# Sums of the V weights' blocks placed sooner; one add for four heads' exponentials, and the first unit's block sums between the rotary products

## The chip, the cores and the metric

The kernel runs on one core of one Trainium2 chip. A core has five engines, each with its own queue of instructions that it works through in order: TensorE (PE in the profile), VectorE (DVE), ScalarE (ACT), GpSimd (POOL) and SyncE (SP, which here issues the DMAs). They wait for each other on semaphores. The metric is the device time of one execution in microseconds. The kernel before took 2176.2 us (median of three runs, 2175.44 to 2180.79).

## The reference

Two transformer layers follow each other on 16 sequences of 256 tokens and 256 channels, all in float32. Each layer has self-attention, cross-attention to a context, and a feed-forward block, every one behind a layer norm whose factor and shift come from a condition vector. Layer 0 has 16 heads of 64 channels with rotary turns of the queries and keys; layer 1 has 16 heads of 16 channels. Cut to what matters here, the attention of layer 0 is:

```python
def _attn(xq, ctx, wq, wkv, wo, bo):
    q = _heads(xq @ wq)
    k, v = jnp.split(ctx @ wkv, 2, axis=-1)
    k = _heads(k)
    v = _heads(v)
    q = _rope(q, sq, cq)
    k = _rope(k, sk, ck)
    sim = jnp.einsum('bhnd,bhmd->bhnm', q, k) * DH ** (-0.5)
    a = jax.nn.softmax(sim, axis=-1)
    o = jnp.einsum('bhnm,bhmd->bhnd', a, v)
    return o.transpose(0, 2, 1, 3).reshape(xq.shape[0], xq.shape[1], MID) @ wo + bo
```

In the self-attention of layer 0 `ctx` is the normed input itself, so V is the product of a 256 x 256 input and a 256 x 1024 matrix of weights.

## The kernel before, in words

The work is cut into 96 jobs: six phases (layer 0 self-attention, cross-attention, feed-forward, then the same of layer 1) of 16 sequences each. A job of attention has two steps, s = 0 and s = 1; a step handles two units of four heads. The loop over `steps` writes the instructions of every engine out in an order made by hand, and nothing reorders them: an instruction stands in its engine's queue where the loop puts it, and what it needs from other engines it waits for.

**A step of layer 0.** At its end the step before has put the scores of this step's two units into PSUM (`scores`, `stage_s`, matmuls of line 657), and ScalarE takes their exponentials, two heads at a time (line 670), so that a unit has two tiles `pr` of 128 x 1024. The denominators of the softmax come by VectorE: `stage_t` adds the two halves of the keys of two heads (line 679, one add for each `pr`), `stage_turn` transposes the sum in blocks of 32 (line 685), `stage_reduce` sums each block (line 692). TensorE meanwhile makes the queries and keys of the next step in four parts, `rotary(then, e, half)`, with e the unit. After each part VectorE multiplies the result by cosines and sines (two instructions of line 614, tiles `m`), and after the second part of a unit GpSimd makes the turned queries and keys, tiles `qk`, by one subtraction and one addition (line 622). There are two buffers for each kind of `m`, so the second unit's multiplications wait until GpSimd has read the first unit's. `layer0_sums` multiplies the exponentials with V (line 727). Then `scores` of the next step follows: it overwrites the PSUM banks that the rotary products stood in, so it needs all eight multiplications of line 614, and `qk` of both units.

**Order of VectorE in a step**, where nothing else comes between: add, add, transpose of the first unit; two multiplications; first add of the second unit; two multiplications; second add; four multiplications; block sums of the first unit; transpose and block sums of the second. After that in s = 1 come the additions to the residual `x` (lines 1018 to 1025, in `finish_folded`, for the job before) and the norm of a later job (lines 364 and 374); in s = 0 the moments of a later one.

**Seven products in place of eight.** In the first phase V of jobs 2 and later is made with Strassen's scheme (`by_seven`, `value_part`): seven block products with sums of blocks of the weights and of the tokens. The sums of the weights are made once, by four GpSimd instructions (`fold_value_weights`, lines 519 to 522; one of them writes over a block of `wv` itself, so the plain products of jobs 0 and 1 must be done). Five more sums, of blocks of the output weights, are made once in a phase (`fold_weights`, line 995), for `finish_folded`. Both calls stand at the end of step s = 1 of job 0. The sums of the tokens are made for each job (`fold_tokens`, lines 532 to 535) at the head of step s = 0 of the job before. TensorE's second product in that step (`value_part(nxt, 0)`, block product 5) needs the first of them.

**Buffers.** The tiles with tag `pr` come from four buffers of 128 x 1024; the feed-forward jobs take theirs, `sums` in `pair_hidden`, from the same four.

Of the kernel before, what the change touches and what calls it, by code (L numbers as in the profile page):

```python
# [10 lines left out]
F32 = mybir.dt.float32  # L11
# [32 lines left out]
def fast(ctx: ExitStack, tc: tile.TileContext, a: dict, out: bass.AP, flag):  # L44
# [222 lines left out]
    def wtile(shape, tag, name, bufs=1):  # L267
        return wpool.tile(shape, F32, tag=tag, name=name, bufs=bufs)
# [375 lines left out]
    def stage_s(job, u, at):  # L644

        key = job["key"]
        pair = job["qk"].pop(u)
        for t in range(NT):
            for half in range(2 if job["layer"] == 0 else 1):
                for g, h in [(g, h) for g in range(2) for h in range(4)]:  # L650
                    r = slice(32 * h, 32 * h + 32)
                    keys = slice(t * P + 64 * g, t * P + 64 * g + 64)
                    if job["layer"] == 0:
                        lhs, rhs = pair[half][r, 1, keys], pair[half][r, 0, :]
                    else:
                        lhs, rhs = pair[1][r, keys], pair[0][r, :]
                    nc.tensor.matmul(  # L657
                        banks[64 * g : 64 * g + 64, at + h, t * N : (t + 1) * N], lhs, rhs,
                        start=(half == 0 and (t == 0 or job["layer"] == 1)),
                        stop=(half == 1 or job["layer"] == 1), skip_group_check=(job["layer"] == 0),  # L660
                    )
        prs = []
        for p in range(2):
            pr = work.tile([P, 2, NT, N], F32, tag="pr", name=f"pr_{key}_{u}_{p}", bufs=4)
            sc = banks[:, at + 2 * p : at + 2 * p + 2, :].rearrange("p h (t n) -> p h t n", n=N)

            parts = 2 if job["layer"] == 1 and u % 2 == 0 and p == 0 else 1
            for i in range(parts):
                one = slice(i, i + 1) if parts == 2 else slice(0, 2)
                nc.scalar.activation(pr[:, one], sc[:, one], AF.Exp, scale=0.125 if job["layer"] == 0 else 0.25)  # L670
            prs.append(pr)
        job["pr"][u] = prs

    def stage_t(job, u, p):

        pr = job["pr"][u][p]
        if p == 0:
            job["both"] = work.tile([P, 4, N], F32, tag="both", name=f"both_{job['key']}_{u}", bufs=1)
        nc.vector.tensor_tensor(job["both"][:, 2 * p : 2 * p + 2, :], pr[:, :, 0, :], pr[:, :, 1, :], ALU.add)  # L679

    def stage_turn(job, u):

# [35 lines left out]

    def layer0_sums(job, u, at):

        key, v, prs = job["key"], job["v"], job["pr"].pop(u)
        o = bank(at, 2, N)
        for half in range(2):
            for t in range(NT):
                for h in range(4):
                    col = (4 * u + h) * 64 + 32 * half
                    nc.tensor.matmul(  # L727
                        o[32 * h : 32 * h + 32, half, :], v[:, t, col : col + 32], prs[h // 2][:, h % 2, t, :],
                        start=(t == 0), stop=(t == NT - 1),
                    )  # L730
        if u % 2 == 0:
            job["halves"].append(work.tile([P, 4, N], F32, tag="part", name=f"raw_{key}_{u}", bufs=4))
        raw = job["halves"][-1][:, 2 * (u % 2) : 2 * (u % 2) + 2, :]
        nc.scalar.copy(raw, o)  # L734
        job["raw"].append(raw)

    def layer1_sums(job, c, e, at):

        key, v, prs = job["key"], job["v"], job["pr"].pop(2 * c + e)
        o = bank(at, N)  # L740
        for t in range(NT):
            for h in range(4):
                nc.tensor.matmul(  # L743
                    o[32 * h : 32 * h + 32], v[:, t, 4 * c + h, 32 * e : 32 * e + 32],
                    prs[h // 2][:, h % 2, t, :], start=(t == 0), stop=(t == NT - 1),
                )

        if c == 0 and e == 0:  # L750
            job["parts"].append(work.tile([P, 4, N], F32, tag="part", name=f"oT_{key}", bufs=4)[:, 0:2, :])
            job["sums"] = work.tile([P, N], F32, tag="inv", name=f"sums_{key}")
        raw, sums = job["parts"][0][:, c, :], job["sums"]
        if e == 0:
            nc.scalar.activation(raw, o, AF.Copy, scale=mask[:, 0:1])
        else:
            nc.vector.scalar_tensor_tensor(raw, o, mask[:, 1:2], raw, ALU.mult, ALU.add)
        eighth = mask[:, 4 - 2 * e + c : 5 - 2 * e + c]
        if c == 0 and e == 0:
            nc.scalar.activation(sums, o, AF.Copy, scale=eighth)  # L760
        else:
            nc.vector.scalar_tensor_tensor(sums, o, eighth, sums, ALU.mult, ALU.add)
# [99 lines left out]
    def pair_hidden(job, pair, part):  # L862
# [3 lines left out]
        mine = slice(2 * half, 2 * half + 2)  # L866
        if part == 0:
            job["places"] = x, y, z = [bank(next_bank(), 2, N) for _ in range(3)]
            job["sums"] = [work.tile([P, 2, 2, N], F32, tag="pr", name=f"sums{i}_{key}", bufs=4) for i in range(2)]
            copy, six = (job["sums"][0][:, i] for i in range(2))  # L870
            block_products(job, x, 1, True)
            block_products(job, y, 6, True)
            block_products(job, z, 5, True)
            nc.scalar.copy(copy, x)
            nc.vector.tensor_tensor(six, y, copy, ALU.add)
            if half == 0:
                for one in pair:
# [9 lines left out]
        copy, six = (job["sums"][0][:, i] for i in range(2))  # L887
        seven = job["sums"][1][:, 0]
# [95 lines left out]
        for t in (1, 0):  # L984
            nc.sync.dma_start(out=out[job["b"]][t * P : (t + 1) * P], in_=x[:, t, :])

    def fold_weights(ph):
        w = ph["w"]["wo"]
        b = [[w[:, 4 * k : 4 * k + 4, n * P : (n + 1) * P] for n in range(2)] for k in range(2)]
        folded = ph["folded"] = {2: b[0][0], 5: b[1][1]}  # L990
        for m, x, y, op in ((1, b[0][0], b[1][1], ALU.add), (3, b[0][1], b[1][1], ALU.subtract),
                            (4, b[1][0], b[0][0], ALU.subtract), (6, b[0][0], b[0][1], ALU.add),
                            (7, b[1][0], b[1][1], ALU.add)):
            folded[m] = wtile([P, 4, P], "folded", f"folded_w_{m}", 5)
            nc.gpsimd.tensor_tensor(folded[m], x, y, op)  # L995

# [175 lines left out]
    for i, (j, s) in enumerate(steps):  # L1172
# [123 lines left out]
        elif layer0:  # L1296
            then = attention(i + 1, 0)
            if leaving and s == 1 and nxt["kind"] == "ffn":
                fold_input_weights(nxt["phase"], nc.gpsimd)
            if s == 0 and by_seven(nxt):  # L1300
                fold_tokens(nxt, nc.gpsimd)
                stage_t(job, 0, 0)
                stage_t(job, 0, 1)
                stage_turn(job, 0)
                rotary(then, 0, 0)
                stage_t(job, 1, 0)
                rotary(then, 0, 1)
                sum_up(late, 5)
                if make_mod:
                    make_mod["mod"] = make_mod["make_mod"](6)  # L1310
                value_part(nxt, 0)
                stage_t(job, 1, 1)
                rotary(then, 1, 0)
                value_part(nxt, 1)
                rotary(then, 1, 1)
                stage_reduce(job, 0)
                value_part(nxt, 2)
                layer0_sums(job, 0, 5)
                value_part(nxt, 3)
# [2 lines left out]
                value_part(nxt, 4)  # L1322
                stage_reduce(job, 1)
            else:
                stage_t(job, 2 * s, 0)
                stage_t(job, 2 * s, 1)
                stage_turn(job, 2 * s)
                rotary(then, 0, 0)
                stage_t(job, 2 * s + 1, 0)
                rotary(then, 0, 1)  # L1330
                if late is not None and s == 1 and then:
                    fold_inner(late, nc.gpsimd, 7, 6)
# [13 lines left out]
                stage_reduce(job, 2 * s + 1)  # L1346
            if late is not None and s == 1:
# [14 lines left out]
            else:  # L1362
# [657 lines left out]
```

## Time and profile before

| what | value |
| --- | --- |
| median of three runs | 2176.2 us (2175.44 to 2180.79) |
| the profiled execution, its own time | 2174.1 us |
| its span, first to last instruction | 2172.3 us |
| TensorE's mean granted clock | 0.997 |
| TensorE busy | 2145.4 us of the span |
| VectorE, ScalarE, GpSimd busy | 1701.7, 878.2, 1282.5 us |
| adds of exponentials (line 679) | 256, mean 875 ns |
| GpSimd's `qk` (line 622) | 256, mean 1382 ns |
| block sums (line 692) | 128, mean 1213 ns |

The profile is one execution. A line of a timeline gives start and duration in microseconds, engine, source line, operation, tiles written and read, their shapes, how many instructions of the kind follow each other, and in square brackets how long the engine sat idle before and what released it. A view of waits adds such idle times up by the pair of waiting and releasing line: total, number, longest. A merged row runs from its first instruction's start to its last one's end, so the row itself says where its engine was next free. Spans of GpSimd are rough.

### The profile page before, as it was taken

To read this page: it belongs to the slowest core of one execution; us is meant where nothing else is said; L and a number is where in the kernel's file an instruction comes from. 1 tells how busy PE (TensorE), PEld (TensorE's weight loads), DVE (VectorE), ACT (ScalarE), POOL (GpSimd) and SP (SyncE) were. 2 spreads that over 40 slices of the span, in tenths; PEclk is the share of its full clock that TensorE was granted. 3 is DMA by queue.
4 is the path that set the end of the run, shared out by engine and by line. 5 is a ranking of instruction groups with operands and counts; after the bars stand their busy time and mean duration, and the time that the engine had idled before them with its cause. 6 is when DMAs were issued, how large, how long until landed. Compare 5 with 4: busy or idle time off the path is not lost.

```text
span 2172.3 us, 110056 instructions
## 1 busy us (share of the span) xinstructions
PE 2145.4 (99%) x50000; PEld 1412.5 (65%) x50000; DVE 1701.7 (78%) x3136; ACT 878.2 (40%) x1376; POOL 1282.5 (59%) x1234
## 2 busy tenths in 40 slices
PE   9899999999999999999999999999999999999998
PEld 5466666666665665666666667877565656566887
DVE  6687887877888999888889887774777777777875
ACT  3233333333333233333333334443666666665442
POOL 3766767767766867677676767662222323335673
PEclk9999999999999999999999999999999999999999
DMA  6011011011124221121211123221221232223221
GB/s 194 24 28 37 23 28 37 23 28 37 26 66 113 66 55 47 40 62 35 59 42 43 43 60 99 58 44 24 66 43 38 49 102 62 52 53 81 73 66 39
DMA packets 307029, 117.67 MB, mean 54 GB/s; under 512 B 243364, under 2 KB 289784, under 8 KB 306424
## 3 DMA queue, kind: packets, MB, share of 16 engines
q1 hardware_dynamic: 306008, 110.02, 20.5%
q8 instruction: 393, 6.44, 1.3%
q14 instruction: 84, 0.69, 0.1%
q10 hardware_dynamic: 544, 0.52, 0.1%
HBM read 77.14 MB, written 33.29 MB: 51 GB/s over the span
## 4 chain that ended last, share of the span: by engine, by line
PE 89%; DVE 4%; POOL 3%; DMA 1%; issue 1%; SPq 1%; ACT 0%; DVEq 0%; POOLq 0%; ACTq 0%
PE banks L82 57%; PE banks L657 15%; PE banks L727 9%; PE banks L743 5%; PE banks L593 1%; PE banks L502 1%; DVE m L614 1%; POOL raw L716 1%; POOL qk L622 1%; POOL folded L929 0%; DMA spread<-sums_seen 0%; DMA fetched<-turned 0%; SPq L214 0%; POOL folded_w L995 0%; POOL folded L1004 0%
## 5 line engine op out<-in xcount | busy, mean ns | idle before, releaser
L670 ACT ACTIVATE pr<-banks 128x1024 f32<-128x1024 f32 x576 | 487.5, 937 | 426.2 <-PE banks L657 222.4
L622 POOL TENSOR_TENSOR qk<-m,m 128x512 f32<-128x512 f32 x256 | 348.4, 1382 | 268.4 <-DVE m L614 245.6
L614 DVE TENSOR_TENSOR m<-banks,rope 128x512 f32<-128x512 f32 x512 | 324.7, 679 | 118.0 <-POOL qk L622 74.2
L679 DVE TENSOR_TENSOR both<-pr 128x512 f32<-128x512 f32 x256 | 221.4, 875 | 39.6 <-ACT pr L670 39.5
L657 PE MATMUL banks<-qk 32*64 32x256 f32 x8192 | 240.8, 378 | 2.9 <-DVE x L1021 2.0
L727 PE MATMUL banks<-pr,v 128*32 128x256 f32 x4096 | 236.2, 379 | 0.0
L734 ACT COPY raw<-banks 128x512 f32<-128x512 f32 x128 | 75.2, 587 | 390.4 <-PE banks L727 378.2
L657 PEld LDWEIGHTS banks<-qk 32*64 32x64 f32 x8192 | 184.8, 131 | 62.9 <-issue 28.1
L727 PEld LDWEIGHTS banks<-pr,v 128*32 128x32 f32 x4096 | 133.2, 110 | 100.5 <-issue 16.8
L716 POOL TENSOR_TENSOR raw<-raw,spread 128x512 f32<-128x512 f32 x128 | 161.5, 1297 | 13.4 <-DMA spread<-sums_seen 13.1
L785 POOL TENSOR_TENSOR oT<-oT,spread 128x256 f32<-128x256 f32 x64 | 45.7, 736 | 206.2 <-DVE spread L784 206.2
L685 DVE STREAM_TRANSPOSE squares<-both 128x1024 f32<-128x1024 f32 x128 | 159.3, 1244 | 3.9
L692 DVE TENSOR_REDUCE rows<-squares 128x32 f32<-128x1024 f32 x128 | 155.3, 1213 | 1.7
L452 POOL TENSOR_TENSOR x<-x,bo_b 128x256 f32<-128x256 f32 x96 | 72.8, 778 | 121.5 <-DVE xh L364 121.5
L1004 POOL TENSOR_TENSOR folded<-raw,raw 128x512 f32<-128x512 f32 x90 | 138.7, 1568 | 2.4
L82 PE MATMUL banks<-hT,wk_sa 128*32 128x256 f32 x2048 | 135.2, 382 | 0.1
L82 PE MATMUL banks<-hT,wq_ca 128*32 128x256 f32 x2048 | 134.4, 379 | 0.0
L743 PE MATMUL banks<-pr,wide_v 128*32 128x256 f32 x2048 | 134.3, 379 | 0.0
L82 PE MATMUL banks<-hT,wq_sa 128*32 128x256 f32 x2048 | 133.9, 379 | 0.0
L960 DVE TENSOR_TENSOR x<-banks,x 128x256 f32<-128x256 f32 (+2 forms) x150 | 79.6, 531 | 63.0 <-PE banks L82 56.8
L657 PE MATMUL banks<-q,k 32*64 32x256 f32 x4096 | 128.3, 381 | 0.0
L356 POOL TENSOR_TENSOR rstd<-ve,neg_half 128x2 f32<-128x2 f32 x95 | 67.6, 711 | 99.4 <-DVE ve L354 95.7
(246 smaller groups left out, 4047.4 us busy)
## 6 DMA issues: line engine op xcount, KB each, us to landing
turned<-blocks SPq DMA_DIRECT2D x380, 64.0 KB
fetched<-turned SPq DMA_DIRECT2D x380, 64.0 KB
spread<-sums_seen SPq DMA_DIRECT2D x128, 128.0 KB
x<-in_x SPq DMA_DIRECT2D x16, 256.0 KB
fetched_c<-turned_c SPq DMA_DIRECT2D x64, 64.0 KB
cT<-in_ctx_turned SPq DMA_DIRECT2D x16, 256.0 KB
out<-x SPq DMA_DIRECT2D x15, 256.0 KB
ctx<-in_ctx SPq DMA_DIRECT2D x16, 192.0 KB
```

What stands on the lines that cost most here:

```text
L82: nc.tensor.matmul(out[cut], lhsT[:, cut], rhs, start=start, stop=stop, **more)
L614: nc.vector.tensor_tensor(m, pq, rope[:, s : s + 1, :].to_broadcast([P, 2, N]), ALU.mult)
L622: nc.gpsimd.tensor_tensor(r, x, y, (ALU.subtract, ALU.add)[out])
L657: nc.tensor.matmul(banks[64 * g : 64 * g + 64, at + h, t * N : (t + 1) * N], lhs, rhs, start=(half == 0 and (t == 0 or job["layer"] == 1)) ...
L670: nc.scalar.activation(pr[:, one], sc[:, one], AF.Exp, scale=0.125 if job["layer"] == 0 else 0.25)
L679: nc.vector.tensor_tensor(job["both"][:, 2 * p : 2 * p + 2, :], pr[:, :, 0, :], pr[:, :, 1, :], ALU.add)
L685: nc.vector.transpose(job["squares"].rearrange("p b k -> p (b k)"), job.pop("both").rearrange("p h n -> p (h n)"))
L692: nc.vector.tensor_reduce(job["rows"][:, u, :], job.pop("squares"), AX.X, ALU.add)
L716: nc.gpsimd.tensor_tensor(part, part, spread[:, u : u + 1, :].to_broadcast([P, 2, N]), ALU.mult)
L727: nc.tensor.matmul(o[32 * h : 32 * h + 32, half, :], v[:, t, col : col + 32], prs[h // 2][:, h % 2, t, :], start=(t == 0), stop=(t == NT - 1),
L743: nc.tensor.matmul(o[32 * h : 32 * h + 32], v[:, t, 4 * c + h, 32 * e : 32 * e + 32], prs[h // 2][:, h % 2, t, :], start=(t == 0), stop=(t ...
L1004: eng.tensor_tensor(folded[m], *sums[m])
```

## The change

Three things are done.

The exponentials of a unit get one tile of 128 x 2048 in place of two (two buffers of it in place of four of half the size; `sums` of the feed-forward jobs likewise), and `stage_t` adds the two halves of the keys for all four heads in one instruction. ScalarE's exponentials stay as they are. In the order of a step, the one add of the second unit stands where its second add stood.

`stage_reduce` of the first unit is put directly behind the second unit's add, ahead of `rotary(then, 1, 0)`.

`fold_value_weights`, and two of the five sums of `fold_weights`, for the first phase, are put at the head of step s = 1 of job 0 in place of its end. The other three stay there. In the second phase all five stay.

```diff
-        prs = []
+        whole = job["pr"][u] = work.tile([P, 4, NT, N], F32, tag="pr", name=f"pr_{key}_{u}")
         for p in range(2):
-            pr = work.tile([P, 2, NT, N], F32, tag="pr", name=f"pr_{key}_{u}_{p}", bufs=4)
+            pr = whole[:, 2 * p : 2 * p + 2]
...
-    def stage_t(job, u, p):
-
-        pr = job["pr"][u][p]
-        if p == 0:
-            job["both"] = work.tile([P, 4, N], F32, tag="both", name=f"both_{job['key']}_{u}", bufs=1)
-        nc.vector.tensor_tensor(job["both"][:, 2 * p : 2 * p + 2, :], pr[:, :, 0, :], pr[:, :, 1, :], ALU.add)
+    def stage_t(job, u):
+
+        pr = job["pr"][u]
+        both = job["both"] = work.tile([P, 4, N], F32, tag="both", name=f"both_{job['key']}_{u}", bufs=1)
+        nc.vector.tensor_tensor(both, pr[:, :, 0, :], pr[:, :, 1, :], ALU.add)
...
-            job["sums"] = [work.tile([P, 2, 2, N], F32, tag="pr", name=f"sums{i}_{key}", bufs=4) for i in range(2)]
-            copy, six = (job["sums"][0][:, i] for i in range(2))
+            job["sums"] = work.tile([P, 4, 2, N], F32, tag="pr", name=f"sums_{key}")
+            copy, six = (job["sums"][:, 2 * i : 2 * i + 2, 0, :] for i in range(2))
...
-    def fold_weights(ph):
+    def fold_weights(ph, which):
...
+            if m not in which:
+                continue
...
+            if job["p"] == 0 and job["b"] == 0 and s == 1:
+                fold_value_weights(job["phase"], nc.gpsimd)
+                fold_weights(job["phase"], (1, 3))
             if s == 0 and by_seven(nxt):
                 fold_tokens(nxt, nc.gpsimd)
-                stage_t(job, 0, 0)
-                stage_t(job, 0, 1)
+                stage_t(job, 0)
                 stage_turn(job, 0)
                 rotary(then, 0, 0)
-                stage_t(job, 1, 0)
                 rotary(then, 0, 1)
                 sum_up(late, 5)
...
                 value_part(nxt, 0)
-                stage_t(job, 1, 1)
+                stage_t(job, 1)
+                stage_reduce(job, 0)
                 rotary(then, 1, 0)
                 value_part(nxt, 1)
                 rotary(then, 1, 1)
-                stage_reduce(job, 0)
                 value_part(nxt, 2)
...
             else:
-                stage_t(job, 2 * s, 0)
-                stage_t(job, 2 * s, 1)
+                stage_t(job, 2 * s)
                 stage_turn(job, 2 * s)
                 rotary(then, 0, 0)
-                stage_t(job, 2 * s + 1, 0)
                 rotary(then, 0, 1)
...
-                stage_t(job, 2 * s + 1, 1)
+                stage_t(job, 2 * s + 1)
+                stage_reduce(job, 2 * s)
                 rotary(then, 1, 0)
                 rotary(then, 1, 1)
...
                 for e in range(2):
                     layer0_sums(job, 2 * s + e, 4 + e if then else e)
-                stage_reduce(job, 2 * s)
                 stage_turn(job, 2 * s + 1)
                 stage_reduce(job, 2 * s + 1)
...
                 if job["b"] == 0:
-                    fold_weights(job["phase"])
-                    if job["p"] == 0:
-                        fold_value_weights(job["phase"], nc.gpsimd)
+                    fold_weights(job["phase"], (4, 6, 7) if job["p"] == 0 else (1, 3, 4, 6, 7))
```

The matmuls that read exponentials (`layer0_sums`, `layer1_sums`) read the same elements out of the larger tile.

More of the change, by code (lines that the diff above doesn't have):

```diff
@@ L670, in stage_s @@
                 nc.scalar.activation(pr[:, one], sc[:, one], AF.Exp, scale=0.125 if job["layer"] == 0 else 0.25)
-            prs.append(pr)
-        job["pr"][u] = prs
-    def stage_t(job, u, p):
-        pr = job["pr"][u][p]
-        if p == 0:
-            job["both"] = work.tile([P, 4, N], F32, tag="both", name=f"both_{job['key']}_{u}", bufs=1)
-        nc.vector.tensor_tensor(job["both"][:, 2 * p : 2 * p + 2, :], pr[:, :, 0, :], pr[:, :, 1, :], ALU.add)
+    def stage_t(job, u):
+        pr = job["pr"][u]
+        both = job["both"] = work.tile([P, 4, N], F32, tag="both", name=f"both_{job['key']}_{u}", bufs=1)
+        nc.vector.tensor_tensor(both, pr[:, :, 0, :], pr[:, :, 1, :], ALU.add)
     def stage_turn(job, u):
@@ L719, in layer0_sums @@
     def layer0_sums(job, u, at):
-        key, v, prs = job["key"], job["v"], job["pr"].pop(u)
+        key, v, pr = job["key"], job["v"], job["pr"].pop(u)
         o = bank(at, 2, N)
@@ L727, in layer0_sums @@
                     nc.tensor.matmul(
-                        o[32 * h : 32 * h + 32, half, :], v[:, t, col : col + 32], prs[h // 2][:, h % 2, t, :],
+                        o[32 * h : 32 * h + 32, half, :], v[:, t, col : col + 32], pr[:, h, t, :],
                         start=(t == 0), stop=(t == NT - 1),
@@ L737, in layer1_sums @@
     def layer1_sums(job, c, e, at):
-        key, v, prs = job["key"], job["v"], job["pr"].pop(2 * c + e)
+        key, v, pr = job["key"], job["v"], job["pr"].pop(2 * c + e)
         o = bank(at, N)
@@ L744, in layer1_sums @@
                     o[32 * h : 32 * h + 32], v[:, t, 4 * c + h, 32 * e : 32 * e + 32],
-                    prs[h // 2][:, h % 2, t, :], start=(t == 0), stop=(t == NT - 1),
+                    pr[:, h, t, :], start=(t == 0), stop=(t == NT - 1),
                 )
@@ L886, in pair_hidden @@
         x, y, z = job["places"]
-        copy, six = (job["sums"][0][:, i] for i in range(2))
-        seven = job["sums"][1][:, 0]
+        copy, six = (job["sums"][:, 2 * i : 2 * i + 2, 0, :] for i in range(2))
+        seven = job["sums"][:, 0:2, 1, :]
         (top, bottom), (top2, bottom2) = ([h[:, mine, :] for h in one["halves"]] for one in pair)
@@ L985, in finish_last @@
             nc.sync.dma_start(out=out[job["b"]][t * P : (t + 1) * P], in_=x[:, t, :])
-    def fold_weights(ph):
+    def fold_weights(ph, which):
         w = ph["w"]["wo"]
         b = [[w[:, 4 * k : 4 * k + 4, n * P : (n + 1) * P] for n in range(2)] for k in range(2)]
-        folded = ph["folded"] = {2: b[0][0], 5: b[1][1]}
+        folded = ph.setdefault("folded", {2: b[0][0], 5: b[1][1]})
         for m, x, y, op in ((1, b[0][0], b[1][1], ALU.add), (3, b[0][1], b[1][1], ALU.subtract),
```

## The prediction

> **What bounds the kernel now.** I read the page's busy times first, then the waits of TensorE, then the timelines around the waits that are long.
>
> ```profile
> PE 2145.4 (99%) x50000; PEld 1412.5 (65%) x50000; DVE 1701.7 (78%) x3136; ACT 878.2 (40%) x1376; POOL 1282.5 (59%) x1234
> ```
>
> ```profile
> PE banks L82 <- POOL tokens L532: 10.8, 1, 10.8
> PE banks L657 <- DVE x L1021: 2.0, 2, 1.0
> ...
> PE banks L657 <- DVE x L1025: 0.6, 2, 0.3
> ```
>
> TensorE is busy for all but 27 us of the 2172.3 us span, and the change takes no matmul away. So it can gain only what TensorE waits. One wait, met once, is 10.8 us: for the first sum of the tokens' blocks. The next two rows belong together: at 682.9 and 839.98 us the scores waited 1.0 us for an addition to the residual, and 0.3 us more for a later one, 1.3 us each time. The rest is the start, the end, and single waits that no edit touches.
>
> The timelines of GpSimd and TensorE show what the long wait hangs on:
>
> ```profile
> 60.41 2.52 POOL L622 TENSOR_TENSOR qk<-m,m 128x512 f32<-128x512 f32 x2 [1.49 <-DVE m L614]
> 64.30 1.53 POOL L452 TENSOR_TENSOR x<-x,bo_sa 128x256 f32<-128x256 f32 x2 [1.38 <-DVE xh L364]
> 65.81 1.52 POOL L426 TENSOR_SCALAR hT<-fetched,fac_a,add_a 128x256 f32<-128x256 f32 x1
> 67.29 7.07 POOL L995 TENSOR_TENSOR folded_w<-wo_sa 128x512 f32<-128x512 f32 x5
> 74.33 1.26 POOL L519 TENSOR_TENSOR sums_of_weights<-wv_sa 128x512 f32<-128x512 f32 x1
> ...
> 78.34 1.26 POOL L522 TENSOR_TENSOR sums_of_weights<-wv_sa,sums_of_weights 128x512 f32<-128x512 f32 x1
> 79.56 0.45 POOL L532 TENSOR_TENSOR tokens<-hT 128x128 f32<-128x128 f32 x1
> ```
>
> ```profile
> 68.23 1.04 PE L82 MATMUL banks<-wv_sa,hT 128*32 128x512 f32 x8
> 80.07 1.93 PE L82 MATMUL banks<-wv_sa,tokens 128*32 128x512 f32 x8 [10.79 <-POOL tokens L532]
> ```
>
> TensorE was ready at 69.28 us. GpSimd had nine sums of weights ahead of the tokens, from 67.29 to 79.6 us. In steady state nothing of this kind shows: the jobs of the first phase follow each other every 40.46 us and those of the second every 38.42 us (most of the pieces in the chain of work repeat at that distance).
>
> **The V weights' sums, and two of the five others, moved.** At the new place GpSimd has done its work of step 0 at 46.1 us (the small power of line 356) and sits idle until the `qk` of 56.10 us, 10.0 us by that row's bracket. Six sums start there. They follow each other every 1.33 us (74.33, 75.66, 77.00, 78.34), so they end at 46.1 + 6 x 1.33 = 54.1 us, before that `qk`. One of them overwrites a block of V weights: TensorE's last plain product with it ended at 46.8 us, and this sum is the second, at 47.4 us. They issue no DMA, and SP's queue is not passed. What is left behind `hT` is three sums.
>
> They are not quite alone. VectorE's add of exponentials and GpSimd's sums get in each other's way:
>
> ```profile
> 50.99 0.69 DVE L679 TENSOR_TENSOR both<-pr 128x512 f32<-128x512 f32 x1 [0.22 <-ACT pr L670]
> ...
> 71.74 1.51 DVE L679 TENSOR_TENSOR both<-pr 128x512 f32<-128x512 f32 x1
> ```
>
> The first ran with GpSimd idle, the second beside a sum of weights. In the second case GpSimd's sum ended at 72.70, the add at 73.25, and the next sum took 1.70 us where its neighbours took 1.26 to 1.28: first one works, then the other. So each add costs GpSimd roughly its own length, and waits itself for at most one GpSimd instruction.
>
> Now the sum. In step 1 of job 0 the first add starts when the second exponential is done, 50.97 us, waits for a sum (to about 51.4), and ends at about 52.6; transpose 1.2, four multiplications 2.4, second add 1.2, block sums 1.2, four multiplications 2.5: the last multiplication ends at 61.2 to 61.9 us, where it ended at 60.23. TensorE's scores begin at 61.05 us now, so they wait up to 0.9 us, and `qk` of the second unit comes about 1.1 us later. This is not added to the path, since GpSimd's chain ends later still: `x` at 64.1 to 64.5, then 1.53, then `hT` and the next job's first add after one another, to about 67.5; three sums of 1.28 to 71.3; the second add, 1.2, which by the rows above gets in before the tokens; 0.45 for the tokens: TensorE can go on at 73.0 us where it went on at 80.07. That gains **7.0 us**. If the second add comes behind the first tokens, it is 8.3; if another 1 us of adds falls on GpSimd, 6.0. TensorE is then still waiting about 2.5 us there. Behind this place everything moves up together: the reciprocals' transfer (`spread`) is needed about 7 us sooner, but it was issued at about 72 us and its readers began at 91.6.
>
> **The one add of four heads.** No row shows an add of 128x1024. From below: the block sums over as many elements, with one input, take 1.21 us; from above: two adds, 1.34 us alone, or 3.34 us for a pair beside GpSimd (1014.83 us). Alone I take the lower end, 1.2 us, as the nearest row. So VectorE saves about 0.14 us on a unit, 128 units, 18 us in all, on an engine that is not the bound. In return the first add waits for the second exponential, which comes 0.9 us after the first. Neither is worth anything by itself: TensorE waits for no add of this kind, it reads the exponentials themselves.
>
> **Block sums between the rotary products.** They stand where VectorE now sits idle until GpSimd has read the first unit's `m`, and the four multiplications behind them are what the next scores need:
>
> ```profile
> 1024.19 2.54 DVE L614 TENSOR_TENSOR m<-banks,rope 128x512 f32<-128x512 f32 x4 [1.18 <-POOL qk L622]
> ...
> 1027.85 2.52 POOL L622 TENSOR_TENSOR qk<-m,m 128x512 f32<-128x512 f32 x2
> ...
> 1031.24 3.71 PE L657 MATMUL banks<-qk 32*64 32x256 f32 x128
> ```
>
> The idle time is 1.18 us, the block sums 1.21. From the end of the second pair of multiplications to the end of the last took 4.32 us (1022.41 to 1026.73); it becomes 1.2 + 1.2 + 2.5 = 4.9, that is 0.6 more, or up to 1.2 if GpSimd's `qk` is held up by the whole add. Against that the second pair ends sooner, as one add of 0.67 is gone from ahead of it. So the multiplications end between 0.7 us sooner and 1.2 us later. They have 4.5 us to the scores here, and `qk` of the second unit ends at 1030.37, 2.7 us before the second half of the scores at 1033.1; no repeated step has less. Nothing is lost there.
>
> What follows the multiplications on VectorE comes sooner, for the 1.2 us of block sums are gone from there. That is what the two waits of 1.3 us are for. In both steps the addition stands at the end of multiplications, block sums, transpose, block sums. At 675.20 the multiplications waited 3.73 us for `qk`, so add and block sums fit in, and the addition is 1.2 us sooner; at 832.26 they waited 1.18, and it is 0.6 to 1.3 sooner. I take both as 1.2 saved, **2.4 us**; at the least 1.0, at the most 2.6.
>
> One step has no room: step 0 of the last job of cross-attention of layer 0, with no V products of a next job between sums and scores. TensorE waited 0.27 us there for `qk` (1278.67). Its multiplications ended at 1275.95; worked through as above they end 0.2 to 1.5 us later, and I take 0.6: **minus 0.6 us**.
>
> The Trainium skill, page "SBUF — State Buffer", section "Who interferes with whom", says that a VectorE instruction with two inputs in SBUF and a GpSimd instruction that reads SBUF lock each other out, whichever starts first keeping the shared port for its whole length. The 1.51 and 1.70 us above agree. It speaks against one long add: it would hold `qk` for all of 1.2 us where the 0.63 us add now costs it 0.5 (3.06 against 2.53 us for the pair at 284.96). By that rule the last step loses 1.5 in place of 0.6, and the whole gain is 7.9.
>
> **The larger tile.** Both halves of a unit are read up to the same four matmuls, so one buffer of twice the size comes free when the two did; `sums` likewise. Nothing gained or lost.
>
> **Sum.** 7.0 + 2.4 - 0.6 = 8.8 us, so the profiled execution's 2174.1 becomes 2165.3. The median of the runs shown stands 2.1 us above that execution, and I add the difference: 2167.4.
>
> **Rivals.** *Only the long wait shrinks* (0.22): the lock holds `qk` for the whole add in every step, VectorE's tail comes no sooner, the two waits stay, the last step loses 1.5: 7.0 - 1.5 = 5.5 us gained, 2170.7. For it: 0.6 and 1.2 are nearly one size. Against it: the idle 3.73 us at 675.20 is there to be filled. *The sums can't start early* (0.03): if something not seen kept GpSimd from them until about 50 us, `qk` would start 2 us late and the scores with it, 4 us gained, 2172. Against it: 10.0 us idle and all inputs loaded long before. *The second unit's multiplications come too late in every step* (0.05): the place is `qk` of the second unit in the step s = 1 of cross-attention, fifteen times; it decides from 2.7 us of delay on, and each further us costs 15. At 3.7 us of delay 15 us are lost against 8.8 gained, 2182.4. Against it: I find 1.2 us at the most.
>
> **Numbers.** The forecast has 0.70; its own ends are 6.0 + 1.0 - 1.5 = 5.5 and 8.3 + 2.6 - 0.2 = 10.7 gained, 2165.5 to 2170.7. Runs of one kernel lie some 2 us apart (2174.1 to 2176.2, one higher), which I add below: 2163 to 2171, taking in the first rival. A difference of 0.3%, 6.5 us, is about what can be told from none. Of the forecast 0.70 and of the first rival 0.07 gain more: faster 0.77; the rest of the first rival and the second, 0.18, the same; the third, 0.05, slower.
>
> **What will show it.** TensorE's wait for `tokens` should be 1 to 4 us in place of 10.8, and six sums of GpSimd stand between 46 and 55 us. The add of 128x1024 should have a median near 1.2 us. The two waits for the residual should be gone or under 0.5 us, and the wait for `qk` near 1270 grow to about 0.9 us. The jobs' distances of 40.46 and 38.42 us should stay. If a distance grew, the third rival holds; if the long wait stayed above 5 us, the second; if a new wait came up in every job of layer 0, I have missed who stands behind the add.

## The result, and the profile after

The changed kernel took 2162.94 us (median of four runs, 2162.62 to 2164.62), the kernel before 2175.82 us in the same comparison (four runs, 2175.31 to 2180.79): a ratio of 0.9942, 95% interval 0.9929 to 0.9955. By the medians 12.9 us were gained, by the two profiled executions 11.5 us (2174.1 to 2162.62). The forecast had 8.8 us and 2167.4 us. The measured median stands at the low edge of the range given (2163 to 2171), 0.06 us under it, and both gains are larger than the 10.7 us that the forecast's own terms allowed at most.

The page's busy times, and from the view of TensorE's waits the rows that answer to those of before:

```profile
PE 2141.6 (99%) x50000; PEld 1411.8 (65%) x50000; DVE 1656.1 (77%) x3008; ACT 878.3 (41%) x1376; POOL 1323.4 (61%) x1234
```

```profile
PE banks L82 <- POOL tokens L532: 2.3, 1, 2.3
...
PE banks L82 <- ACT pr L670: 1.3, 2, 1.2
...
PE banks L657 <- POOL qk L622: 0.5, 2, 0.3
...
PE banks L657 <- DVE x L1024: 0.3, 1, 0.3
```

The wait for tokens went from 10.8 to 2.3 us. Of the waits for the residual 0.3 us is left. A new one stands there: 1.2 us for exponentials, at one place. VectorE has 128 instructions less and 46 us less work. GpSimd's busy time grew by 41 us with the same number of instructions; 29 us of it are `qk`'s, of a mean of 1494 ns in place of 1382, since its spans hold more waiting beside the longer add.

Next, how far the same matmuls of TensorE came forward, by the starts in both timelines:

| TensorE reaches | before, us | after, us | sooner by |
| --- | --- | --- | --- |
| scores at the end of the first step | 46.92 | 46.40 | 0.52 |
| scores behind the first seven products | 93.55 | 83.88 | 9.67 |
| first keys behind the first wait for the residual | 685.76 | 674.50 | 11.26 |
| first keys behind the second | 842.82 | 828.58 | 14.24 |
| scores of layer 1's first job | 1497.18 | 1483.10 | 14.08 |
| the projection behind them | 1499.09 | 1486.26 | 12.83 |
| layer 1's feed-forward, third pair | 1988.66 | 1977.28 | 11.38 |
| end | 2172.3 | 2160.8 | 11.5 |

The first 0.52 us is the start of the run (input rows that landed sooner), not the change. So the kernel gained 9.15 us around the V sums and some 4.6 us in the attention of layer 0, and lost 1.25 us at layer 1's start and about 1.3 us in the last phase. In between the jobs follow each other as before, every 40.46 us in the first phase and every 38.42 us in the second. GpSimd around the V sums, after:

```profile
43.89 1.28 POOL L519 TENSOR_TENSOR sums_of_weights<-wv_sa 128x512 f32<-128x512 f32 x1
45.78 1.27 POOL L520 TENSOR_TENSOR wv_sa<-wv_sa 128x512 f32<-128x512 f32 x1 [0.61 <-PE banks L82]
...
49.72 3.52 POOL L994 TENSOR_TENSOR folded_w<-wo_sa 128x512 f32<-128x512 f32 x2
55.88 3.38 POOL L622 TENSOR_TENSOR qk<-m,m 128x512 f32<-128x512 f32 x2 [2.65 <-DVE m L614]
...
63.48 1.52 POOL L452 TENSOR_TENSOR x<-x,bo_sa 128x256 f32<-128x256 f32 x2 [0.23 <-DVE xh L364]
64.99 1.53 POOL L426 TENSOR_SCALAR hT<-fetched,fac_a,add_a 128x256 f32<-128x256 f32 x1
66.48 3.75 POOL L994 TENSOR_TENSOR folded_w<-wo_sa 128x512 f32<-128x512 f32 x3
70.19 1.45 POOL L532 TENSOR_TENSOR tokens<-hT 128x128 f32<-128x128 f32 x1
```

The six sums stand where GpSimd was idle, and still leave it 2.65 us before `qk`. They begin at 43.89 us, sooner than the 46.1 of the forecast (with the V sums alone it is 46.45): step 0's block sums had moved too, so what stands behind them, down to the small power of line 356, came sooner. The second of them did wait, 0.61 us, for TensorE's last plain product with the block that it overwrites. The pair of 49.72 took 3.52 us, not 2.6, and the first tokens 1.45 us, not 0.45: in each an add of VectorE stood beside it. TensorE behind the wait:

```profile
71.69 1.06 PE L82 MATMUL banks<-wv_sa,tokens 128*32 128x512 f32 x8 [2.32 <-POOL tokens L532]
72.57 1.05 PE L82 MATMUL banks<-hT,wk_sa 128*32 128x256 f32 x16
```

Before, those eight products took 1.93 us (a row that the prediction shows) and the next sixteen 1.51. The view by stretches of time gives the granted clock behind PE, PEld, DVE, ACT and POOL's busy times. Before:

```profile
80.00:81.00 1.00, 0.93 (x8) 0.28 (x12) 0.00 (x0) 0.00 (x0) 0.92 (x4) 0.50 0.00 0
...
83.00:84.00 1.00, 1.00 (x28) 0.53 (x24) 0.00 (x0) 0.00 (x0) 0.83 (x1) 1.00 0.00 0
```

and after:

```profile
72.00:73.00 1.00, 1.00 (x16) 0.39 (x12) 0.45 (x1) 0.00 (x0) 1.00 (x4) 1.00 0.18 62
```

So the long wait had a second cost. TensorE went on at half its clock until 82.7 us: from the wait's end to the scores it took 13.48 us (80.07 to 93.55), after the change 12.19 (71.69 to 83.88), 1.29 us less.

VectorE in the step of the second wait for the residual, after:

```profile
816.37 1.20 DVE L676 TENSOR_TENSOR both<-pr 128x1024 f32<-128x1024 f32 x1
817.50 1.21 DVE L689 TENSOR_REDUCE rows<-squares 128x32 f32<-128x1024 f32 x1
818.76 2.53 DVE L614 TENSOR_TENSOR m<-banks,rope 128x512 f32<-128x512 f32 x4
...
824.39 0.69 DVE L1020 TENSOR_TENSOR x<-banks,x 128x512 f32<-128x512 f32 x1
```

Add and block sums stand without a gap ahead of the four multiplications, and the addition to the residual ends at 825.08 us, where TensorE's scores had started at 824.95.

The new wait, in ScalarE's timeline of before and then of after:

```profile
1495.19 1.28 ACT L670 ACT_TABLE_LOAD   x1
1498.35 3.83 ACT L670 ACTIVATE pr<-banks 128x512 f32<-128x512 f32 x5 [1.89 <-PE banks L657]
```

```profile
1484.32 1.28 ACT L670 ACT_TABLE_LOAD   x1 [3.23 <-PE banks L657]
1485.61 3.84 ACT L670 ACTIVATE pr<-banks 128x512 f32<-128x512 f32 x5
```

The table of the exponential is loaded between the last Gelu of layer 0 and the first exponential of layer 1. Before, the load ran in idle time and the exponential waited for the scores; now the load itself stands behind that wait.

### The profile page after: what moved, and what is told of

Its sections match the earlier page's. It is cut to its first block, busy times and chain, and to the rows that moved or that the text cites. A ratio compares the mean times of both kernels' runs of the same rounds, so it can differ in the third digit from the quotient of the medians.

```text
span 2160.8 us, 109747 instructions
## 1 busy us (share of the span) xinstructions
PE 2141.6 (99%) x50000; PEld 1411.8 (65%) x50000; DVE 1656.1 (77%) x3008; ACT 878.3 (41%) x1376; POOL 1323.4 (61%) x1234
## 4 chain that ended last, share of the span: by engine, by line
PE 93%; POOL 3%; DVE 2%; DMA 1%; SPq 1%; issue 1%; ACT 0%; POOLq 0%; DVEq 0%; ACTq 0%
PE banks L82 59%; PE banks L657 16%; PE banks L724 10%; PE banks L740 5%; PE banks L593 2%; PE banks L502 1%; POOL qk L622 1%; POOL folded L926 0%; SPq L389 0%; DVE m L614 0%; DMA fetched<-turned 0%; POOL folded L1003 0%; POOL folded_w L994 0%; SPq L379 0%; POOL raw L713 0%
## 5 line engine op out<-in xcount | busy, mean ns | idle before, releaser
L622 POOL TENSOR_TENSOR qk<-m,m 128x512 f32<-128x512 f32 x256 | 377.1, 1494 | 212.9 <-DVE m L614 205.6
L614 DVE TENSOR_TENSOR m<-banks,rope 128x512 f32<-128x512 f32 x512 | 319.5, 678 | 37.7 <-PE banks L82 24.8
L676 DVE TENSOR_TENSOR both<-pr 128x1024 f32<-128x1024 f32 x128 | 172.3, 1346 | 104.2 <-ACT pr L670 102.3
```

What stands on the lines that cost most here:

```text
L614: nc.vector.tensor_tensor(m, pq, rope[:, s : s + 1, :].to_broadcast([P, 2, N]), ALU.mult)
L622: nc.gpsimd.tensor_tensor(r, x, y, (ALU.subtract, ALU.add)[out])
L676: nc.vector.tensor_tensor(both, pr[:, :, 0, :], pr[:, :, 1, :], ALU.add)
```

## The experiments

Each was run in turn with the kernel before on the same chip; the median of that one is given with it. The ratio, with its 95% interval, is estimated from all runs of both, so it is not exactly the quotient of the two medians. Where a difference is under 2 us, the runs' scatter hides it, and the place in the trace decides.

**The V sums alone.**

```diff
+            if job["p"] == 0 and job["b"] == 0 and s == 1:
+                fold_value_weights(job["phase"], nc.gpsimd)
+                fold_weights(job["phase"], (1, 3))
...
-                    fold_weights(job["phase"])
-                    if job["p"] == 0:
-                        fold_value_weights(job["phase"], nc.gpsimd)
+                    fold_weights(job["phase"], (4, 6, 7) if job["p"] == 0 else (1, 3, 4, 6, 7))
```

> Before, with only the four V sums and two of the five others moved to the head of step 1 of job 0. My account: TensorE's wait for the first tokens falls from 10.8 us to 2 to 3.5 us, and its clock stays at full speed behind it, so by the fourth job's start some 9.3 us are gained (8 from the wait, 1.3 from the clock); the two waits for the residual (1.3 us each by the profile) stay, and nothing changes in layer 1. Time 9 to 10 us under before. Rival, that the port lock of the old, shorter adds eats the gain: 6 to 7 us.

2167.93 us against 2177.75, ratio 0.996 (0.9946 to 0.9974). TensorE's waits:

```profile
PE banks L82 <- POOL tokens L532: 2.9, 1, 2.9
PE banks L82 <- DVE inner L843: 2.6, 1, 2.6
...
PE banks L657 <- DVE x L1023: 1.1, 2, 0.8
```

By the medians 9.8 us were gained, as expected. The long wait falls as in the whole change, and the waits for the residual stay, though smaller. In the profiled execution the clock didn't stay full: its record shows half clock for 3.41 us at this place, and so 7.2 us were gained by the scores there, not the 9.3 expected. Another 2.4 us went at 1977 us, in the last phase, where a wait of 2.6 us for `inner` met a second spell of 3.41 us; no part of the edit is near. The five runs agree with a clock that differs from one execution to the next: at a mean granted clock of 1.000 they took 2166.39 and 2167.0 us, at 0.999 2167.93, at 0.998 2168.76 (the profiled one) and 2169.32.

**The block sums alone.**

```diff
+                stage_reduce(job, 2 * s)
                 rotary(then, 1, 0)
                 rotary(then, 1, 1)
...
-                stage_reduce(job, 2 * s)
```

and likewise in the branch of the seven products.

> Before, with only the block sums of the first unit moved ahead of the second unit's rotary products; two adds for each unit as before, V sums late. My account: the additions to the residual come about 1.2 us sooner, both waits of TensorE for them vanish, 3 to 4 us gained; the long wait of 10.8 us stays. Rival, that the block sums only take the place of idle time if the adds are one instruction: 0 to 1 us gained, the waits stay.

2170.3 us against 2177.75, ratio 0.997 (0.996 to 0.9979). TensorE's waits:

```profile
PE banks L82 <- POOL tokens L532: 9.7, 1, 9.7
...
PE banks L657 <- DVE x L1025: 0.3, 1, 0.3
```

The waits for the residual are gone but for 0.3 us with two adds, so the rival falls. The gain is more than the 3 to 4 us expected: 7.5 us by the medians, 4.6 us by the two profiled executions, from behind the run's start to TensorE's last product. The trace puts 1.26 us of it at the first of the two waits and 2.21 at the second; and 0.76 us between 749 and 762 us and 0.67 us in the first phase, in steps where the view of waits shows no idle time before.

**The one add alone.** The larger tile and the one add, as in the change; block sums and V sums as before.

> Before, with only one tile for four heads and one add; block sums and V sums where they were. My account: VectorE saves time but nobody waits for it: the two waits for the residual shrink by less than 0.7 us each, and the first exponentials of layer 1 get the 1.2 us wait of TensorE that the changed kernel shows (the load of the exponential's table standing behind the wait for the scores). Between 1 us faster and 1.5 us slower than before. Rival, that the add is what frees VectorE: 2 us or more faster.

2176.97 us against 2177.75, ratio 1.0001 (0.9992 to 1.0011). TensorE's waits:

```profile
PE banks L82 <- POOL tokens L532: 11.1, 1, 11.1
PE banks L82 <- ACT pr L670: 1.3, 2, 1.2
...
PE banks L657 <- DVE x L1020: 0.9, 1, 0.9
```

Nothing gained, as expected, and the wait for exponentials comes with it: it belongs to this part of the change. At the second wait for the residual it did gain 1.6 us, more than the 0.7 expected; the new wait, a longer wait for tokens and smaller delays ate that.

**The feed-forward sums in one piece.** The first guess at the new wait was the layout of the three sums that share the tiles' two buffers.

```diff
-            copy, six = (job["sums"][:, 2 * i : 2 * i + 2, 0, :] for i in range(2))
+            copy, six = (job["sums"][:, i] for i in range(2))
...
-        seven = job["sums"][:, 0:2, 1, :]
+        seven = job["sums"][:, 2]
```

> The changed kernel, with the feed-forward jobs' three sums laid one behind the other in their tile in place of interleaved. Theory: at the start of layer 1 the first exponentials overlap ScalarE's own copy only in part, so that they wait for it as well as for TensorE, and the wait for TensorE is put ahead of the table's load; in one piece the load comes back ahead of the wait, TensorE's wait of 1.2 us there vanishes: about 1.2 us under the changed kernel, 2161.7. Rival, that the larger tile's turn in the two buffers is what does it: the wait of 1.2 us stays and the time is the same.

2163.15 us against 2177.75, ratio 0.9939 (0.9922 to 0.9956). The guess falls:

```profile
PE banks L82 <- ACT pr L670: 1.3, 2, 1.2
```

The semaphores that the traces record with each instruction say more. Before, the table's load had no wait and the first exponential one, for TensorE. After, that exponential waits on ScalarE's own semaphore, and the wait for TensorE stands ahead of the load; in this experiment it is the same. With two tiles and two adds (below) it is as before. The second wait is not for VectorE, so it comes with the tile and not with the add; whether the rival's turn in the two buffers brings it is not shown.

**The table early.** One exponential of a column of ones, ahead of the first projections of layer 1, on the changed kernel.

```diff
                 if then:
+                    soon = stat.tile([P, 1], F32, tag="ve", name="exponential_soon")
+                    nc.scalar.activation(soon, ones, AF.Exp)
                     stage_a(then[0], 0, next_bank())
```

> The changed kernel with one exponential of 128x1 on ScalarE ahead of the last feed-forward step of layer 0's end, so that the exponential's table is loaded before the scores of layer 1. Theory: the load stands behind the wait for TensorE only because the first exponential has got a second wait (for ScalarE's own earlier work); loaded sooner, TensorE's wait of 1.2 us for those exponentials goes and the time falls by about 1.2 us, to 2161.7. Rival, that the exponentials are late for another reason, as their buffer: the wait stays and the time is the same.

2161.84 us against 2174.78, ratio 0.9937 (0.9924 to 0.9951); too near to the changed kernel's 0.9942 to tell by time. ScalarE's timeline:

```profile
1484.17 1.28 ACT L1284 ACT_TABLE_LOAD   x1
1485.46 0.20 ACT L1284 ACTIVATE exponential_soon<-ones 128x1 f32<-128x1 f32 x1
1485.57 0.59 ACT L422 ACTIVATE hT<-fetched,add_b,fac_b 128x256 f32<-128x256 f32 x1
1487.88 3.83 ACT L670 ACTIVATE pr<-banks 128x512 f32<-128x512 f32 x5 [1.73 <-PE banks L657]
```

The load is out of the wait, TensorE's wait for `pr` is gone from its list, and the matmuls behind this place came 1.25 us forward against the changed kernel. That settles what the wait was. This execution lost 1.8 us at the tokens instead: their wait was 2.3 us as in the changed kernel, but the clock fell to half for 3.41 us.

**Two adds kept.** The changed kernel with the old two tiles and two adds.

> The changed kernel with the old two tiles and two adds: V sums early and block sums early, but no add of four heads. Theory: the one add is worth little and its tile costs 1.2 us at the start of layer 1; so this is as fast as the changed kernel or up to 1.5 us faster (2161.5 to 2163), unless the wait for tokens, 2.9 us with two adds, brings a spell of half clock as it did once with the V sums alone, which gives 1 us back. Rival, that the one add gains on its own by shorter locks between VectorE and GpSimd: 2 us or more slower than the changed kernel.

2160.77 us against 2174.78, ratio 0.9933 (0.9919 to 0.9946). The wait for tokens:

```profile
PE banks L82 <- POOL tokens L532: 1.8, 1, 1.8
```

Without the one add it is as fast or a little faster (2 us by the two ratios, whose intervals overlap): 1.21 us sooner at layer 1's start, and the tokens come 0.5 us sooner, since what stands beside them is shorter.

**The tokens first.** With the early table, and the last three sums of output weights out of the tokens' way:

```diff
                 rotary(then, 0, 1)
+                if job["p"] == 0 and job["b"] == 1:
+                    fold_weights(job["phase"], (4, 6, 7))
                 sum_up(late, 5)
...
-                    fold_weights(job["phase"], (4, 6, 7) if job["p"] == 0 else (1, 3, 4, 6, 7))
+                    fold_weights(job["phase"], () if job["p"] == 0 else (1, 3, 4, 6, 7))
```

> As the one with the early table, and the last three sums of output weights moved from ahead of the first tokens to behind the next qk, in job 1. Theory: GpSimd's idle time between the two qk of that step (4 us) takes them, so TensorE's last 2.3 us of waiting for tokens go: 3 to 3.5 us under the changed kernel, about 2159.5. Rival, that they now hold up the second qk or the first adds there and TensorE waits for the scores: 1.2 us under the changed kernel or less.

2157.95 us against 2174.78, ratio 0.9924 (0.991 to 0.9937). The wait for tokens isn't in TensorE's list any more. Against the changed kernel it is 3.9 us by the ratios, a little more than expected.

**The tokens first, with two adds.** The same without the one add, and so without the early table.

> V sums at the head of step 1 of job 0, the last three of the five others behind the next qk, block sums early, and the old two adds and two tiles (so that the exponential's table needs no early load). Theory: the one add is worth nothing on TensorE's path, so this takes as long as the same with one add and the early table: 2156.5 to 2159.5. Rival, that the one add helps by itself once nothing else is late: 2 us or more slower than that, over 2160.

2157.11 us against 2173.62, ratio 0.9922 (0.9908 to 0.9935). GpSimd and TensorE:

```profile
66.53 0.46 POOL L532 TENSOR_TENSOR tokens<-hT 128x128 f32<-128x128 f32 x1
...
70.95 2.71 POOL L622 TENSOR_TENSOR qk<-m,m 128x512 f32<-128x512 f32 x2 [2.57 <-DVE inv L701]
73.62 3.77 POOL L997 TENSOR_TENSOR folded_w<-wo_sa 128x512 f32<-128x512 f32 x3
77.35 2.52 POOL L622 TENSOR_TENSOR qk<-m,m 128x512 f32<-128x512 f32 x2
```

```profile
69.25 1.04 PE L82 MATMUL banks<-wv_sa,tokens 128*32 128x512 f32 x8
```

The three sums fit between the two `qk`, and TensorE doesn't wait. The two kernels with the tokens first are the fastest of this study and can't be told apart: the one add is worth nothing once its 1.2 us of table load are mended. By the ratios both are 3.9 to 4.4 us ahead of the changed kernel (0.9942), though the intervals overlap; by the traces 2.5 us of that are gained at the tokens and 1.1 to 1.2 us at layer 1's start.

**The wait filled.** To see the clock by itself: the kernel before, with products of the identity put where TensorE waits. Nothing reads them.

```diff
             value_product(job, 1, 6, True)
+            if job["p"] == 0 and job["b"] == 2:
+                for _ in range(40):
+                    nc.tensor.matmul(
+                        bank(4, 2, P), ident, ident.unsqueeze(1).to_broadcast([P, 2, P]), start=True, stop=True
+                    )
             value_product(job, 5, 4, True)
```

> Before, with 40 products of the identity put on TensorE into the free bank where it waits for the first tokens of the third job; they are extra work that nothing reads. Theory: before, TensorE's granted clock fell to half about 3 us into the wait of 10.8 us and stayed there until 2.6 us after its end, which cost 1.3 us beyond the wait. With TensorE kept busy the record shows no half clock there, the 48 products behind the wait take their usual 3 to 3.9 us in place of 4.1 to 5, and the scores of that step come about 1.3 us sooner after the wait's end than before. Rival, that the products behind the wait are slow for another reason (their inputs just written, VectorE or GpSimd beside them): they stay slow at full clock.

2177.63 us in a single run, beside 2174.78. The 40 products took 17.5 us, 6 us more than the wait, so the time says nothing. But the clock stayed full, and from the first product with tokens to the scores it took 12.20 us (86.19 to 98.39).

**Half of it filled**, with 20 products.

> Before, with half as many extra products in the wait, 20 in place of 40, since 40 took 17.5 us, 6 us longer than the wait. These should end at about 77.5 us and leave TensorE some 2 us of waiting for the tokens. Theory of the clock: no spell of half clock at this place, or one of 3.4 us at the most; from the wait's end to the scores of that step 12.2 us in place of 13.5, so 0.5 to 1.3 us under before. Rival, that nothing but the wait itself counts: 13.5 us stay, the time is that of before.

2173.79 us against 2173.62, ratio 1.0 (0.9991 to 1.0009): 1.3 us can't be told from none. At the place it can:

```profile
79.30 1.06 PE L82 MATMUL banks<-wv_sa,tokens 128*32 128x512 f32 x8 [2.01 <-POOL tokens L532]
80.19 1.05 PE L82 MATMUL banks<-hT,wk_sa 128*32 128x256 f32 x16
```

1.06 us where the kernel before took 1.93 for the same eight products, full clock, and 12.20 us to the scores (79.30 to 91.50) in place of 13.48. With the same sums ahead of the tokens, the 1.3 us are the clock's. The loss grows with the spell as it should: in the kernel before half clock lasted 2.65 us beyond the wait's end and cost 1.28 us against 12.20, with the one add alone it lasted 5.72 us beyond it and cost 2.80 (15.00 us, 80.06 to 95.06), each time about half.

## Why the prediction was right, and where not

**The long wait.** Right in kind and in place; the last of the terms were a little long. I had TensorE going on at 73.0 us; allowing for the start, that is 72.5, and it was 71.69. The wait fell by 8.47 us, less 0.61 lost at the late scores of step 1, together 7.9 against the 7.0 forecast. With the same allowance, `hT` ended at 66.5 us, not at 67.0, and the three sums behind it at 70.2, not 70.8; the first tokens were held by VectorE's add as forecast, 1.45 us. The second rival, that the sums can't start early, falls with their start at 43.89 us.

**The clock: missed.** I had the change gain only what TensorE waits, and put the price of the half clock behind the wait at nothing. I read the row of 80.07 for its bracket and not for its duration: 1.93 us for eight products that take 1.04 in the row of 68.23. The view by stretches also has the clock at 0.69 from 68 to 80 us before the change. 1.29 us of gain were left out.

**The waits for the residual.** Right in mechanism, too small in size: 2.4 us forecast, some 4.6 measured; with the block sums alone the second wait gave 2.2, the first 1.3, and the steps without a visible wait 1.4. I had summed the idle times of TensorE's waits, but matmuls' ends are modelled: at 839.98 us the view shows 0.97 and 0.31 us of idle time, while from the start of the scores to the first keys behind them passed 5.79 us (837.03 to 842.82), after the change 3.63 (824.95 to 828.58).

**The last step of cross-attention.** I forecast 0.6 us lost, or 1.5 by the lock, and a wait for `qk` of 0.9; that wait is 0.3 us as before, and about 0.1 us was lost. The pair of `qk` of the first unit was held longer there (3.57 us, 3.00 before), but the multiplications ended only 0.1 us later: add and block sums took up the 1.16 us that VectorE had waited. The third rival falls as well, since the jobs' distances stayed.

**The one add.** Its duration was right:

```profile
L676 DVE TENSOR_TENSOR both<-pr x128: 1158/1224/2345, 29.4 to 1268.9; 128x1024 f32<-128x1024 f32 x128
```

```profile
L622 POOL TENSOR_TENSOR qk<-m,m x256: 1265/1288/2347, 16.6 to 1263.0; 128x512 f32<-128x512 f32 x128
```

(the columns are shortest, median and longest in ns). The median of 1224 ns is the 1.2 us of the forecast. What VectorE saves by it was not: 18 us forecast, 46 measured, since the two adds before, many of them beside GpSimd, took 875 ns in the mean and not the 0.67 us that each was put at. `qk` at its longest took 2.35 us, 1.06 over its median, where two adds left it at 1.81: it is held for about the length of the add. The Trainium skill, page "SBUF — State Buffer", section "Who interferes with whom", calls the port that the two engines share an exclusive lock, and these rows agree. The margin behind `qk` took that up. The first rival, which let this lock eat VectorE's gain, is wrong: the multiplications behind it had been waiting already.

**The larger tile.** "Nothing gained or lost" is wrong, and it is the step that failed outright: the term was put at nothing. I looked at when its buffers come free, not at what waits the first exponential gets. It cost 1.25 us, once: the load of the table, 1.28 us, stood behind the wait for the scores.

**The last phase.** About 1.3 us were lost in the feed-forward of layer 1 (12.70 us ahead at 1962.08, 11.38 at 1977.28). The change does edit the tile `sums` of these jobs, but the kernel with two adds kept, which has the old tiles, lost 1.4 us there too, so the tile is not what does it. There VectorE and GpSimd meet in a different order: one sum of `inner` took 1.50 us in place of 0.42. The same place cost 2.4 us in the V sums alone, so it varies from kernel to kernel; why it falls so in each is open.

So the sum of 8.8 was short by 0.9 for the wait, 1.3 for the clock, some 2.2 for the block sums and 0.4 for the last step of cross-attention and what follows it, and long by the 1.25 of the table and the 1.3 of the last phase. That makes 11.0 us, and the 0.5 of the start makes the 11.5 of the two profiled executions. That the time still came out at the edge of the range is in part luck: two losses that I had not seen stood against three gains that were larger than I had them.

## What to carry to other kernels

Read the duration of the first instructions behind a long wait as well as the wait: a busy engine's row that is twice its usual length is part of the wait's price. Work that one engine does once belongs where that engine idles, behind nothing that the bound waits for next; here moving three more sums by the same rule took away the 2.3 us that were left. When tiles are merged, look at the list of waits of the first instruction that writes them, above all where a table's load stands ahead of it.

## What the runs showed of the hardware

TensorE's half-clock spells lasted 10.24 us around a wait of 10.8 us (before) and one of 9.7 (the block sums alone), 13.65 around 11.1 (the one add alone), and 3.41 after waits of 2.9 and 2.6 (the V sums alone): whole numbers of 3.41 us. A wait of 2.3 us brought a spell of 3.41 us in the kernel with the early table, and none in the profiled executions of the changed kernel and of the one with the sums in one piece.

The Trainium skill, page "TensorE: Matmul & The Clock Gate", section "What's actually happening", has the clock judged in windows of 3413 ns that run freely, not from the kernel's start. The traces agree: in each, all changes of the clock lie whole numbers of 3.413 us apart. Where they lie against the wait decides. In the changed kernel a border falls into the wait, at 70.55 us:

```profile
67.13:70.55 3.42, 2.23 (x43) 0.84 (x32) 3.38 (x7) 0.57 (x1) 3.42 (x4) 1.00 0.20 33
70.55:73.96 3.41, 2.27 (x36) 1.16 (x40) 1.90 (x2) 0.00 (x0) 3.33 (x5) 1.00 0.29 86
```

With the early table the same wait lies within one stretch:

```profile
68.99:72.41 3.42, 1.10 (x15) 0.16 (x8) 3.37 (x6) 0.57 (x1) 3.34 (x4) 1.00 0.05 6
72.41:75.82 3.41, 3.41 (x28) 1.27 (x24) 0.53 (x1) 0.00 (x0) 3.41 (x5) 0.50 0.57 186
```

(Behind the length of the stretch stands TensorE's busy time; the clock is the third number from the end.) So TensorE idled 1.19 and 1.14 us in two stretches and kept its full clock, or 2.32 us in one and had half of it in the next. All 7571 such stretches of the twelve traces fit. Of the 28 with half clock in the stretch that follows, 27 had 2.24 us or more of idle time, and the one other, with 1.11, was at half clock already (the one add alone, from 78.95 us). None with full clock behind it had more than 1.83. Less than a whole idle stretch is enough, then; where the limit lies between 1.83 and 2.24 us is not shown. The position differs from execution to execution, so that the same wait of 2.3 us costs a spell in one and nothing in another. The changed kernel's runs had a mean clock of 1.000 twice (2162.62 and 2162.66 us), then 0.999 (2163.23) and 0.998 (2164.62).
